# Graph layer on one core: the column lists get tiles of 128 columns of any one set of row groups, and every list product becomes 128x32

## The chip, the core and the metric

One core of a Trainium2 chip. TensorE (PE) multiplies, VectorE (DVE) adds, builds lists and normalises, ScalarE (ACT) evicts, GpSimd (POOL) issues the gathers, SyncE (SP) and ACT issue plain DMAs. The metric is the device time of one execution in microseconds (us), lower is better; a time stands for the median of several runs.

## The reference

x is 8 x 4096 x 256, adj 4096 x 4096, W 256 x 256, all f32.

```python
def reference(x, adj, W):
    HW = einsum('bnf,fo->bno', x, W)
    A_norm = relu((adj + adj.T) * 0.5)
    d = sum(A_norm, axis=1) ** -0.5                  # 0 where the sum is 0
    L_norm = eye(4096) - d[:, None] * A_norm * d[None, :]
    y = relu(einsum('nm,bmo->bno', L_norm, HW))
    return layernorm(x + y, axis=-1)
```

adj is sparse: an entry (i, j) is present with a probability that falls as (1+i)^-0.5 (1+j)^-0.5, so that low-numbered rows and columns are dense and the rest is thin. The kernel must read where the entries are; nothing of adj's pattern is known when it is built except the sizes of tables that are written into the program.

## The kernel before, in words

**Stage 1.** Blocks of 512x512 of adj are loaded (SP queue), transposed on PE (L516), added to their mirror on DVE (L520), relu'd and halved on ACT (L524), and written to a_dram (ACT queue). Sums over 32 columns (DVE L527) tell which group of 32 rows uses which column (`uses`, L528). Beside it x is transposed and multiplied by W; the rows of the result, g (8 batches x 256 = 2048 numbers, 8 KB a row), are scaled and written to g_dram. The first of 32 output blocks of 128 rows (its products are "lead" in the profile), and the lists of the first units, are also made in this stage.

**Stage 2** is the sum over neighbours. It goes through 16 units in the order `SEQ` (1 to 9, 0, 10 to 15). A unit is two output blocks of 128 rows, b = 0 and 1 (unit 15 has one), which are 8 groups of 32 rows. For each output block PE adds, in four PSUM banks (c = 0 to 3, 512 of the 2048 columns of g each), products of a tile of a (128 columns of adj x output rows) with a tile of g (those 128 rows of g). The first 256 columns of adj, the hubs, are always used whole: two hub tiles of g stay in SBUF, and a unit has 4 hub rounds (`g_hub`, `gh`), two for each block. Of the others only the columns that are used are gathered: lists of columns, cut into tiles.

In the kernel before, a list holds the columns of one of 15 fixed kinds (`KINDS`: a single group, some pairs of groups, a whole block, all eight). A list is a number of half-tiles of 64 columns (`CAPS`, `FIRST`), and a tile has two half-tiles. A round of products, which fills PE's 128 columns once for each c, is one 128x128 product, two 128x64, four 128x32, two 64x128 or up to eight 64x32 (rows of the tile x output rows). A catch-all kind takes what is left over; if it too overflows, a slower path behind the kernel runs. With these inputs that doesn't happen, in either kernel.

**The gathers.** For each tile POOL issues two indirect DMAs, `ga` from a_dram (L1032; 128 rows of 128 bytes, 512 bytes or 1 KB, depending on whether the tile serves one group, one block or both) and `g` from g_dram (L1047; up to 128 rows of 8 KB; empty places are skipped). They go into a ring of 12 tiles (`RING`). After each round the program asks for one more tile if the ring has room, for two if it has room for more than 5 (`SLACK`); these gathers wait for the round's last matmul. A ring place comes free in order only: a tile that is still in use holds all behind it. The tile order of the gathers is the order in which the rounds first use them.

**Lists.** Each unit makes steps of the lists of later units. When block 0 of a unit is finished, three of its four PSUM banks are used for counting: positions in the lists of the unit 3 and 4 ahead (L300, L301, L396, L397), and column numbers of the unit 2 ahead (`collect`, L450). DVE reads the counts (L242, L246, L247), and at the end of the unit the column numbers (`index`, L464 and L465); then the banks serve block 0 of the next unit. DVE also adds x to a finished block (L798), takes its moments (L807 to L826) and normalises it (L831); SP stores it.

The loop that orders all this, `for q, (u, step) in enumerate(steps)`, issues the products of a round, then `gather_ahead`, then list work that is due. The order on each engine is the order in which the program is written.

## Time and profile before

| what | value |
|---|---|
| runs | 1496.15, 1495.63, 1490.57 us; median 1495.63 |
| profiled execution, its own time: the span from first to last instruction (nothing lies around it that the profile shows) | 1496.2 us |
| stage 1 | 0 to 587.1 us |
| stage 2, first to last product | 587.1 to 1483.8 us |
| behind it (last block evicted, normalised, stored) | 12.4 us |
| PE / DVE / ACT / POOL busy | 1420.1 / 1025.2 / 368.7 / 745.6 us |
| bytes moved by DMA | 540.52 MB, mean 361 GB/s |

A product is two matmul instructions and two weight loads in the profile, so that a round of 128x128 is 8 matmuls. A window row gives a stretch of time, the busy time of PE, its weight loads, DVE, ACT and POOL in it with instruction counts, the granted PE clock, the mean busy share of the 16 DMA engines, and GB/s. A unit starts with the first hub product of its block 0; unit times below are from one such start to the next, in the order in which the units run:

| unit | 1 | 2 | 3 | 4 | 5 | 6 | 7 | 8 | 9 | 0 | 10 | 11 | 12 | 13 | 14 | 15 |
|---|---|---|---|---|---|---|---|---|---|---|---|---|---|---|---|---|
| us | 75.2 | 72.3 | 62.9 | 58.2 | 56.1 | 55.1 | 52.0 | 52.4 | 48.8 | 97.4 | 48.1 | 51.7 | 55.2 | 48.3 | 41.9 | 21.0 |

### The profile page before, as it was taken

To read this page: it belongs to the slowest core of one execution; us is meant where nothing else is said; L and a number is where in the kernel's file an instruction comes from. 1 tells how busy PE (TensorE), PEld (TensorE's weight loads), DVE (VectorE), ACT (ScalarE), POOL (GpSimd) and SP (SyncE) were. 2 spreads that over 40 slices of the span, in tenths; PEclk is the share of its full clock that TensorE was granted. 3 is DMA by queue.
4 is the path that set the end of the run, shared out by engine and by line. 5 is a ranking of instruction groups with operands and counts; after the bars stand their busy time and mean duration, and the time that the engine had idled before them with its cause. 6 is when DMAs were issued, how large, how long until landed. Compare 5 with 4: busy or idle time off the path is not lost.

```text
span 1496.2 us, 20479 instructions
## 1 busy us (share of the span) xinstructions
PE 1420.1 (95%) x6768; PEld 757.9 (51%) x6768; DVE 1025.2 (69%) x3010; ACT 368.7 (25%) x462; POOL 745.6 (50%) x1547
## 2 busy tenths in 40 slices
PE   7998988979999999999999999999999999998996
PEld 6777877766777764333333334333333333333342
DVE  4767558889596752356569678789898079797454
ACT  4555545434544460010100100100110011001102
POOL 2444010010322336756577677577677646666762
PEclk9999999989999999999999999999999999999998
DMA  9999999999999999979899899999999979988995
GB/s 340 360 377 381 406 346 337 393 385 338 379 356 341 371 392 373 373 270 379 332 377 379 338 402 407 366 388 403 398 382 377 387 259 341 354 316 321 402 404 220
DMA packets 215265, 540.52 MB, mean 361 GB/s; under 512 B 17751, under 2 KB 107527, under 8 KB 180839
## 3 DMA queue, kind: packets, MB, share of 16 engines
q0 software_dynamic: 53808, 281.94, 48.5%
q1 hardware_dynamic: 93200, 126.62, 24.4%
q10 hardware_dynamic: 68144, 130.58, 23.0%
q8 instruction: 56, 0.92, 0.2%
q14 instruction: 57, 0.46, 0.1%
HBM read 425.72 MB, written 136.34 MB: 376 GB/s over the span
## 4 chain that ended last, share of the span: by engine, by line
PE 62%; DMA 14%; DVE 11%; issue 7%; POOL 3%; ACT 3%; ACTq 0%; another core or an unknown queue 0%; DVEq 0%; POOLq 0%; SPq 0%
PE py L1263 45%; PE pg L627 8%; DMA a_dram<-sym 6%; DVE sym L520 4%; DMA g<-g_dram,gi 3%; PE xtr L616 3%; PE lead L585 3%; PE tr L516 3%; DMA xin<-in_x_dram 2%; POOL ga L1032 2%; ACT sym L524 1%; DVE sums L527 1%; POOL g L1047 1%; DMA g_dram<-held 1%; PE lists L450 1%
## 5 line engine op out<-in xcount | busy, mean ns | idle before, releaser
L1263 PE MATMUL py<-g,ga 128*32 128x512 f32 (+4 forms) x2880 | 644.8, 606 | 12.3 <-DMA g<-g_dram,gi 7.2
L1263 PEld LDWEIGHTS py<-g,ga 128*32 128x32 f32 (+4 forms) x2880 | 226.0, 138 | 402.0 <-issue 374.4
L1032 POOL DMA_INDIRECT ga<-a_dram,ai x256 | 277.6, 1084 | 181.3 <-issue 62.2
L1047 POOL DMA_INDIRECT g<-g_dram,gi x256 | 284.5, 1111 | 92.9 <-issue 77.6
L788 ACT ACTIVATE y<-py,minus_r 128x512 f32<-128x512 f32 x120 | 80.2, 686 | 796.3 <-PE py L1263 545.9
L627 PE MATMUL pg<-w_sb,xt 128*128 128x256 f32 x1024 | 233.4, 387 | 6.5 <-ACT xt L617 5.7
L1263 PE MATMUL py<-g_hub,gh 128*128 128x512 f32 x496 | 226.6, 601 | 0.5 <-DVE low L465 0.3
L627 PEld LDWEIGHTS pg<-w_sb,xt 128*128 128x128 f32 x1024 | 196.9, 195 | 34.5 <-ACT xt L617 6.6
L520 DVE TENSOR_TENSOR sym<-tr,adj 128x512 f32<-128x512 f32 x256 | 162.3, 684 | 59.0 <-PE tr L516 54.1
L527 DVE TENSOR_REDUCE sums<-sym 128x64 f32<-128x2048 f32 x64 | 145.7, 2282 | 69.5 <-ACT sym L524 69.5
L528 POOL TENSOR_SCALAR uses<-sums 128x64 uint8<-128x64 f32 x64 | 26.7, 417 | 271.1 <-DVE sums L527 236.9
L516 PE MATMUL tr<-ident,adj 128*128 128x128 f32 x1024 | 137.1, 281 | 20.5 <-DVE sym L520 14.3
L1263 PEld LDWEIGHTS py<-g_hub,gh 128*128 128x128 f32 x496 | 90.5, 190 | 123.6 <-issue 116.8
L524 ACT ACTIVATE sym<-sym 128x2048 f32<-128x2048 f32 x64 | 122.7, 1917 | 122.8 <-DVE sym L520 118.6
L516 PEld LDWEIGHTS tr<-ident,adj 128*128 128x128 f32 x1024 | 115.8, 143 | 50.9 <-DVE sym L520 31.1
L242 DVE TENSOR_TENSOR_SCAN incl_r<-carry,lists 128x32 f32<-128x32 bf16 x13 | 2.9, 221 | 182.0 <-PE lists L397 176.0
L429 DVE TENSOR_TENSOR hot<-iota_q,at 128x1024 bf16<-128x1024 f32 x64 | 74.5, 1220 | 34.0 <-PE lead L585 32.1
L798 DVE TENSOR_TENSOR xr<-xr,y 128x2048 f32<-128x2048 f32 x31 | 70.8, 2284 | 38.8 <-ACT y L788 32.1
L616 PE MATMUL xtr<-ident,xin 128*128 128x128 f32 x512 | 74.5, 299 | 17.9 <-DVE sym L520 9.0
L831 DVE TENSOR_SCALAR xr<-xr,mv,root 128x256 f32<-128x256 f32 x248 | 85.1, 416 | 1.1
L807 DVE BATCH_NORM_STATS2 stats<-xr 128x6 f32<-128x256 f32 x248 | 84.0, 413 | 1.1
L585 PE MATMUL lead<-gt,strip 128*128 128x512 f32 x176 | 82.4, 593 | 0.0
(164 smaller groups left out, 1040.1 us busy)
## 6 DMA issues: line engine op xcount, KB each, us to landing
adj<-in_adj_dram SPq DMA_DIRECT2D x64, 1024.0 KB
a_dram<-sym ACTq DMA_DIRECT2D x64, 1024.0 KB
out_dram<-xr SPq DMA_DIRECT2D x31, 1024.0 KB
xr<-in_x_dram ACTq DMA_DIRECT2D x28, 1024.0 KB
xin<-in_x_dram SPq DMA_DIRECT2D x44, 512.0 KB
g_dram<-gt ACTq DMA_DIRECT2D x22, 1024.0 KB
xin<-in_x_dram POOLq DMA_DIRECT2D x20, 512.0 KB
g_dram<-held ACTq DMA_DIRECT2D x10, 1024.0 KB
```

The lines of the kernel that those rows point to most:

```text
L516: ins = nc.tensor.transpose(pt[:, c * P : (c + 1) * P], tji[:, c, a * P : (a + 1) * P], ident)
L520: nc.vector.tensor_add(sym[:, a, :], pt, tij[:, a, :])
L524: nc.scalar.activation(sym, sym, AF.Relu, scale=0.5)
L527: nc.vector.tensor_reduce(sums, sym.rearrange("p a (c q) -> p a c q", q=E), AX.X, ALU.add)
L585: nc.tensor.matmul(lead[c], lhsT=strip, rhs=g[:, c * S : (c + 1) * S], start=not done, stop=len(done) == NB - 1, skip_group_check=True,)
L616: nc.tensor.transpose(pt[:, k, c, :], xin[b // H][:, b % H + k, c * P : (c + 1) * P], ident)
L627: ins = nc.tensor.matmul(pg[:, k * FO : (k + 1) * FO], lhsT=xt[:, b + k, c, :], rhs=w_sb[:, c, :], start=(c == 0), stop=(c == FC - 1),)
L807: nc.vector.bn_stats(stats[:, b, :], z[:, b, :])
L831: nc.vector.tensor_scalar(z[:, b, :], z[:, b, :], mv[:, b, 0:1], rstd[:, b : b + 1], ALU.subtract, ALU.mult,)
L1032: rows = nc.gpsimd.indirect_dma_start(out=at if both else at[:, : E if one else P], out_offset=None, in_=a_pairs if both else a_groups if ...
L1047: nc.gpsimd.indirect_dma_start(out=gt, out_offset=None, in_=g_dram, in_offset=bass.IndirectOffsetOnAxis(ap=gi[:, t : t + 1], axis=0), boun ...
L1263: return nc.tensor.matmul(py[2 * u + 1 + b][c][cols, :], lhsT=at[ps, off + cols.start : off + cols.stop], rhs=gt[ps, c * S : (c + 1) * S], ...
```

## The change

A table `UNITS` replaces `KINDS`, `CAPS`, `FIRST` and the half-tiles. For each unit it gives: how many full tiles each single group has; the other kinds, each any set of groups as a bit mask, with its number of tiles of 128 columns; the catch-all tiles; the order of the tiles (`turns`); from how many of the next tiles a round may choose (`reach`); and by how much block 1 stands back in that choice (`lag`).

```diff
-KINDS = [15, 1, 4, 2, 8, 16, 64, 32, 128, 240, 51, 204, 60, 195, 0]
-CAPS = [ ... ]
-FIRST = [ ... ]
+UNITS = [
...
+    (
+        [1, 2, 1, 1, 1, 1, 1, 1],
+        [(5, 1, 0), (64, 1, 1), (49, 1, 2), (212, 1, 3), (75, 1, 4), (186, 1, 5)],
+        1,
+        [2, 13, 11, 8, 9, 3, 14, 1, 0, 15, 4, 5, 7, 10, 12, 6],
+        7,
+        8,
+    ),
...
-    REACH = 8
-    SLACK = 5
+    SLACK = 3
-    L = 64
...
+    def match(n, u, pat, k, masks, by):
+        nc.vector.tensor_tensor(beside, pat, masks, ALU.bitwise_and)          # groups that the kind lacks
+        nc.vector.scalar_tensor_tensor(f, beside, 0.0, by, ALU.is_equal, ALU.mult)
+        nc.vector.tensor_reduce(best, f, AX.X, ALU.max)
+        nc.vector.tensor_scalar(best, best, 0.5, None, ALU.max)
+        nc.vector.tensor_tensor(kinds_in[n], f, best, ALU.is_equal)
+        nc.vector.tensor_tensor_scan(ahead_of[n], carry, kinds_in[n], 0.0, ALU.mult, ALU.add)
...
     def lists(u, room):
                 if 3 in ahead[u]:
-                    count_rest(ahead[u][3], pr[:, 0], pr[:, 1])
-                    reads.append(place_rest(ahead[u][3], pr[:, 0], pr[:, 1]))
+                    count_rest(ahead[u][3], pr)
+                    reads.append(place_rest(ahead[u][3], pr))
                 if 4 in ahead[u]:
-                    count(ahead[u][4], tot, low)
-                    reads.append(place(ahead[u][4], tot, low))
+                    count_more(ahead[u][4], q1)
+                    reads.append(place_more(ahead[u][4], q1))
+                if 5 in ahead[u]:
+                    count(ahead[u][5], q0)
+                    reads.append(place(ahead[u][5], q0))
...
     def steps_of(u):
+        out = [full(-1 - h, 0) for h in held] + ([full(-1, 1)] if two else [])
+        while any(todo.values()):
+            near = [t for t in turns if todo[t]][:reach]
+            cells = sorted((op for t in near for op in todo[t]), key=lambda op: turn[op[0]] + lag * op[1])
+            step = []
+            for j in range(QU):
+                step += [op for op in cells if op[2] == j][:1]
+            for op in step:
+                todo[op[0]].remove(op)
+            out.append(step)
+        if two:
+            out += [full(-1 - h, 1) for h in held[1:]]
...
-            for _ in range(room if behind is None else min(room, 1 + (room > SLACK))):
+            for _ in range(room if behind is None else min(room, 1 + room // SLACK)):
                 gather(asked, behind)
...
-                lhsT=at[ps, off + cols.start : off + cols.stop],
-                rhs=gt[ps, c * S : (c + 1) * S],
+                lhsT=at[:, off + cols.start : off + cols.stop],
+                rhs=gt[:, c * S : (c + 1) * S],
```

(The operands of `match` are shortened here.) A column goes to the first kind of the table that holds all its groups, in a first pass over at most 7 kinds and the single groups; what finds no place there is matched again in a second pass, and what then is left goes to the catch-all. So there are three counts for a unit's lists where there were two: 5, 4 and 3 units ahead. Constants come by one DMA from a table in the program, where 752 memsets on POOL wrote them in stage 1. The lists of the first five units are made in stage 1.

What the edit makes of each unit (columns in the lists are the same in both; MB are those columns' 8 KB rows, the `ga` rows, the hub rows, x in and the result out; "ahead" is the least number of tiles that are asked for and not yet begun behind any round of the unit, counted in the program):

| unit | columns | rounds before | after | tiles before | after | MB before | after | least ahead before | after |
|---|---|---|---|---|---|---|---|---|---|
| 1 | 2599 | 20 | 19 | 22 | 23 | 27.1 | 27.3 | 3 | 3 |
| 2 | 2325 | 17 | 17 | 20 | 20 | 24.6 | 24.8 | 6 | 4 |
| 3 | 2128 | 17 | 16 | 19 | 17 | 23.0 | 23.1 | 7 | 1 |
| 4 | 2046 | 15 | 15 | 18 | 17 | 22.2 | 22.3 | 6 | 2 |
| 5 | 1972 | 15 | 14 | 16 | 17 | 21.6 | 21.6 | 7 | 2 |
| 6 | 1855 | 15 | 14 | 15 | 16 | 20.7 | 20.5 | 7 | 4 |
| 7 | 1874 | 14 | 14 | 16 | 15 | 20.6 | 20.8 | 7 | 5 |
| 8 | 1778 | 14 | 13 | 14 | 16 | 19.9 | 19.8 | 7 | 4 |
| 9 | 1652 | 13 | 12 | 14 | 13 | 18.8 | 18.8 | 8 | 7 |
| 0 | 3000 | 27 | 23 | 26 | 24 | 30.9 | 31.1 | 7 | 4 |
| 10 | 1680 | 13 | 13 | 14 | 14 | 19.1 | 19.0 | 7 | 5 |
| 11 | 1594 | 12 | 12 | 15 | 13 | 18.1 | 18.3 | 3 | 3 |
| 12 | 1569 | 12 | 12 | 15 | 13 | 17.9 | 18.1 | 3 | 6 |
| 13 | 1537 | 12 | 12 | 13 | 13 | 17.8 | 17.7 | 6 | 5 |
| 14 | 1505 | 12 | 11 | 12 | 12 | 17.3 | 17.4 | 7 | 6 |
| 15 | 838 | 6 | 5 | 7 | 8 | 10.4 | 10.3 | - | - |
| all | 29952 | 234 | 222 | 256 | 251 | 330 | 331 | | |

In list rounds there were 1440 products, and are 2472. PE, start of unit 3 before, from the last products of its first hub round: a round of four tiles (16 products) stands between it and the second hub round, which follows 12 rows further on. (py_unit_block_c is the PSUM bank of column chunk c; g0 to g11 and ga0 to ga11 are places of the ring; g_hub0 and g_hub1 the two hub tiles.)

```order
L1263 MATMUL py_3_0_1_6884<-g_hub0_5719,gh0_0_5784 128x512
L1263 MATMUL py_3_0_2_6885<-g_hub0_5719,gh0_0_5784 128x512
L1263 MATMUL py_3_0_3_6886<-g_hub0_5719,gh0_0_5784 128x512
L1263 MATMUL py_3_0_0_6883<-g6_5751,ga6_5778 32x512
L1263 MATMUL py_3_0_0_6883<-g7_5755,ga7_5779 32x512
L1263 MATMUL py_3_0_0_6883<-g8_5759,ga8_5780 32x512
L1263 MATMUL py_3_0_0_6883<-g9_5763,ga9_5781 32x512
```

PE, start of the same unit after, from the last product of its first hub round: three hub rounds stand back to back, and then every round is of four 32-wide products.

```order
L1272 MATMUL py_3_0_3_6248<-g_hub0_4943,gh0_0_5008 128x512
L1272 MATMUL py_3_0_0_6245<-g_hub1_4947,gh1_0_5010 128x512
L1272 MATMUL py_3_0_1_6246<-g_hub1_4947,gh1_0_5010 128x512
L1272 MATMUL py_3_0_2_6247<-g_hub1_4947,gh1_0_5010 128x512
L1272 MATMUL py_3_0_3_6248<-g_hub1_4947,gh1_0_5010 128x512
L1272 MATMUL py_3_1_0_6329<-g_hub0_4943,gh0_1_5009 128x512
L1272 MATMUL py_3_1_1_6330<-g_hub0_4943,gh0_1_5009 128x512
L1272 MATMUL py_3_1_2_6331<-g_hub0_4943,gh0_1_5009 128x512
L1272 MATMUL py_3_1_3_6332<-g_hub0_4943,gh0_1_5009 128x512
L1272 MATMUL py_3_0_0_6245<-g7_4979,ga7_5003 32x512
L1272 MATMUL py_3_0_0_6245<-g8_4983,ga8_5004 32x512
L1272 MATMUL py_3_0_0_6245<-g9_4987,ga9_5005 32x512
```

What moved: the second hub round of block 0 and the first of block 1 now stand ahead of the unit's first list round, where a list round parted them; the last of block 1 stands at the unit's end. The tiles in use at one time are 3.2 on the mean over all rounds, where they were 0.9.

DVE, in unit 3, before: what stands between the counts of unit 3's banks (lists0 to lists2) and the moments of its block 0 (L798, the block numbered 7).

```order
L242 SCALAR_TENSOR_TENSOR incl_r6_7145<-carry_96,lists2_3_7140 128x32
L246 TENSOR_TENSOR pos_r6_7147<-incl_r6_7145,lists2_3_7140 128x32
L247 TENSOR_TENSOR pos_r6_7147<-pos_r6_7147,lists2_3_7140 128x32
L242 SCALAR_TENSOR_TENSOR incl_k7_7150<-carry_96,lists0_3_7138 128x448
L246 TENSOR_TENSOR pos_k7_7152<-incl_k7_7150,lists0_3_7138 128x448
L247 TENSOR_TENSOR pos_k7_7152<-pos_k7_7152,lists1_3_7139 128x448
L798 TENSOR_TENSOR xr_7_6999<-xr_7_6999,y_7_7125 128x2048
```

DVE after, the same place from its fourth row on (ahead of these stand L510 and L512, 128x32, and L480, 128x192; behind them L491, then the moments, with L493 behind their first row):

```order
L514 TENSOR_TENSOR pos1_6_6549<-lists2_3_6539,fits1_6_6547 128x32
L481 TENSOR_TENSOR wide_1_at2_7_6552<-lists1_3_6538,begin_7_6054 128x192
L482 TENSOR_TENSOR wide_0_fits2_7_6551<-wide_0_fits2_7_6551,kinds_in_1_113 128x192
L483 TENSOR_TENSOR wide_1_at2_7_6552<-wide_1_at2_7_6552,wide_0_fits2_7_6551 128x192
L485 TENSOR_REDUCE more_7_6557<-wide_1_at2_7_6552 128x32
L434 TENSOR_TENSOR wide_0_fits_8_6567<-lists0_3_6537,tables_99 128x384
L486 TENSOR_TENSOR slot_7_6199<-slot_7_6199,more_7_6557 128x32
L437 TENSOR_TENSOR wide_1_at_8_6568<-lists0_3_6537,tables_99 128x384
L488 TENSOR_SCALAR none2_7_6560<-slot_7_6199 128x32
L445 TENSOR_TENSOR begin_8_6572<-lists0_3_6537,tables_99 128x4
```

What moved: where six rows stood ahead of the moments now fourteen stand, and the column numbers (`index`, L573 and L574 now), whose bank holds up the next unit's fourth hub product, follow the moments as before.

More of the change, by code (lines that the diff above doesn't have):

```diff
@@ L204 @@
[L204 to L225 removed]
+    NT = NE + NM
@@ new lines @@
+    tiles_at = [sum(tiles[:u]) for u in range(NU)]
+    beyond = np.full((NU, NT), 1023, np.int32)
+    limits = np.zeros((NU, NT), np.float32)
+    starts = np.zeros((NU, NT), np.float32)
+    for u, (full, kinds, *_) in enumerate(UNITS):
+        at = 0
+        for g in range(NE):
+            beyond[u, g] = 1023 & ~(1 << g)
+            limits[u, g], starts[u, g] = full[g] * P, at
+            at += full[g] * P
+        for k, (mask, n, first) in enumerate(kinds):
+            beyond[u, NE + k] = 1023 & ~mask
+            limits[u, NE + k], starts[u, NE + k] = n * P, at + first * P
@@ L394, in count_rest @@
[L394 to L410 removed]
+        none = t([P, NB], "none", bufs=1)
@@ L1054, in gather @@
                 )
-            got[u, t] = (at, gt, P if both else 0, one)
+            got[u, t] = (at, gt, who)
         def gather_ahead(behind=None):
```

750 lines of the change are left out of this document (379 added, 371 removed), and 32 rows, old and new, of tables (CAPS, FIRST).

## The prediction

> **What bounds the kernel now.** I read the page first (busy shares, then the DMA tenths by slice), then windows over the two stages and over single units, then PE's groups by shape and its waits, then timelines at a few places.
>
> ```profile
> PE 1420.1 (95%) x6768; PEld 757.9 (51%) x6768; DVE 1025.2 (69%) x3010; ACT 368.7 (25%) x462; POOL 745.6 (50%) x1547
> DMA  9999999999999999979899899999999979988995
> ```
>
> PE is busy for 95% of the span, and DMA is at 90% or more in most slices. The windows say where each of them is the limit: the two stages, then units 1, 2, 7, 11 and 12, then three stretches at DMA's extremes.
>
> ```profile
> 0.00:587.10 587.10, 542.16 (x2894) 423.92 (x2895) 401.05 (x768) 280.70 (x329) 153.12 (x981) 0.97 0.99 368
> 587.10:1483.80 896.70, 877.96 (x3875) 334.00 (x3873) 618.81 (x2217) 83.03 (x125) 587.91 (x563) 0.99 0.95 361
> 587.10:662.34 75.24, 74.87 (x341) 28.18 (x340) 34.51 (x116) 4.54 (x8) 48.34 (x47) 1.00 0.84 314
> 662.34:734.68 72.34, 68.35 (x310) 25.17 (x309) 44.42 (x162) 5.25 (x9) 47.03 (x47) 1.00 0.95 358
> 966.98:1018.97 51.99, 51.62 (x248) 19.89 (x245) 44.25 (x161) 5.62 (x9) 37.90 (x35) 1.00 0.99 376
> 1265.68:1317.40 51.72, 49.85 (x249) 19.59 (x246) 40.55 (x142) 5.53 (x9) 31.33 (x30) 0.97 0.86 308
> 1317.40:1372.60 55.20, 49.48 (x244) 18.58 (x243) 42.72 (x166) 5.50 (x9) 36.38 (x35) 0.94 0.93 338
> 650.00:655.00 5.00, 4.63 (x36) 2.27 (x33) 4.52 (x7) 0.00 (x0) 0.00 (x0) 1.00 0.01 3
> 1000.00:1025.00 25.00, 24.63 (x152) 10.36 (x148) 18.36 (x83) 5.50 (x8) 18.16 (x18) 1.00 1.01 397
> 1025.00:1050.00 25.00, 25.00 (x88) 9.00 (x82) 22.95 (x66) 0.00 (x0) 16.62 (x16) 1.00 1.03 414
> ```
>
> Stage 1 runs at a DMA share of 0.99: the loads of adj set its length. Stage 2 has PE at 878 of 896.7 us and DMA at 0.95 together; neither has much to spare. DMA's full pace is the mean of the last two rows, 0.405 MB/us. Where the ring is full it stands still (share 0.01 at 650), and what it misses there can't be caught up at a pace above full.
>
> A round of products has one price, whatever its shape:
>
> ```profile
> 1018.97 3.60 PE L1263 MATMUL py<-g_hub,gh 128*128 128x512 f32 x8
> 1022.50 3.64 PE L1263 MATMUL py<-g,ga 128*32 128x512 f32 x32
> 1026.07 3.70 PE L1263 MATMUL py<-g_hub,gh 128*128 128x512 f32 x8
> 779.60 5.54 PE L1263 MATMUL py<-g,ga 64*32 64x512 f32 x32
> 784.98 0.18 PE L396 MATMUL lists<-rest,ones 128*128 128x32 bf16 x1
> ```
>
> From start to start a hub round takes 3.53 us, a round of four 128x32 3.57; I take 3.55. A 64x32 round takes 5.38 (779.60 to 784.98), 1.8 more. Unit 7 shows the rest: 51.99 - 14 rounds x 3.55 = 2.3 us for counting and collecting, which all units but the last two have.
>
> So each unit has a floor: the larger of 3.55 x rounds + 2.3 (plus 1.8 in units 1, 2, 11 and 12, for their 64x32 round with all 8 products) and its MB / 0.405. Unit 1: 20 x 3.55 + 2.3 + 1.8 = 75.1 against 27.1/0.405 = 67.0; it took 75.2. With the rounds and MB of the table the floors of before sum to 870.2. The 896.7 measured are 26.5 more, and this is not spread out: units 2, 11, 12 and 13 took 7.9, 5.0, 8.5 and 3.4 us above theirs, 24.8 together. These are the places during or behind the three units in which the least number of tiles ahead falls to 3 (units 1, 11, 12); everywhere else it is 6 or more. A dip to 3 costs 24.8/3 = 8.2 us. The reason shows at unit 12:
>
> ```profile
> 1330.86 9.86 DMA g<-g_dram,gi
> 1351.53 9.82 DMA g<-g_dram,gi
> 1347.93 9.89 PE L1263 MATMUL py<-g,ga 64*32 64x512 f32 x60 [2.80 <-DMA g<-g_dram,gi]
> PE py L1263 <- DMA g<-g_dram,gi: 7.2, 5, 2.8
> ```
>
> In the chain that ended last a gather takes 10 us from issue to landing, nearly three rounds, and then PE waits. PE's own list of waits has only 7.2 us of this; the rest is in matmuls whose modelled ends run long, and in the granted clock (0.94 in unit 12). I price it by unit times, not by waits.
>
> **The change, part by part.** *Fewer rounds.* 234 become 222, and no 64x32 is left: 12 x 3.55 + 4 x 1.8 = 50 us of PE. But in units 5, 8, 9, 11 and 14 DMA's floor now lies above PE's (unit 14: 17.4/0.405 = 43.0 against 11 x 3.55 = 39.1). The floors after sum to 827.9: a gain of 42.3, of which unit 0 alone brings 14.2 (27 to 23 rounds).
>
> *More, smaller products.* 1032 more products, 2064 more matmuls, but four to a round: by the rows above 0.04 us a round for the 128 more rounds of that shape, 5 us at most; against it 125 changes of product shape fewer, of which none shows a price. Between -5 and +5, I take 0: the 3.55 is the mean of both. The Trainium skill (TensorEngine Tiling (Array Packing), Restrictions) speaks against the change here: column tiling switches fast weight load off. By that rule the 32-wide loads would be dearer, and the sum a little above mine; the trace shows no round longer than those 0.04 us.
>
> *The ring.* This is where the gain goes. A tile now serves several rounds, each with four tiles; 3.2 are in use on the mean instead of 0.9, and a place is freed in order only. Of 12 places 7.8 are ahead instead of 8.7. Worse is the rhythm: three hub rounds back to back (10.6 us) use no tile, the ring fills to 11 or 12, POOL has nothing to ask, and DMA drains; then rounds of four new tiles come. What a full ring does is in the trace:
>
> ```profile
> 643.75 1.00 POOL L1047 DMA_INDIRECT g<-g_dram,gi  x1 [0.30 <-issue]
> 655.22 1.11 POOL L1032 DMA_INDIRECT ga<-a_dram,ai  x1 [10.46 <-PE py L1263]
> 656.63 1.00 POOL L1047 DMA_INDIRECT g<-g_dram,gi  x1 [0.30 <-issue]
> 657.93 0.95 POOL L1032 DMA_INDIRECT ga<-a_dram,ai  x1 [0.30 <-issue]
> ```
>
> POOL waits 10.46 us for a product, and then issues a tile each 2.7 us (655.22 to 657.93). A fully used tile is 1.05 MB, 2.6 us at full DMA pace, so asking faster (`SLACK` 3) gains nothing once DMA is full. Price: a dip to 3 is 8.2 us, and each tile less or more is one round, 3.55, more or less: 15.3 for 1, 11.75 for 2, 4.65 for 4, 1.1 for 5. By the table: unit 3 (1) 15.3; units 4 and 5 (2) 23.5; units 1 and 11 (3) 16.4; units 2, 6, 8, 0 (4) 18.6; units 7, 10, 13 (5) 3.3. Together 77.1, so stage 2 takes 827.9 + 77.1 = 905.0, that is +8.3. Bounds: a fixed 8.2 for each of the five dips to 3 or less (41 us, the rivals' case B), and 2.7 us for each late tile (case C). I take the graded price since its steps are those of the rounds. The Trainium skill (DMA: Bandwidth & Descriptors, Anatomy of one DMA — SWDGE (gpsimd) path) has 2.0 us + bytes / 436 GB/s for one such DMA, by which I estimate 4.4 us for a full tile. By it a tile asked two rounds ahead would be in time, the sum would be without this term; the 10 us in the chain, with several gathers sharing the engines, say otherwise.
>
> *The bank handover.* DVE stands between the counts and the next unit's hub round:
>
> ```profile
> L242 DVE TENSOR_TENSOR_SCAN incl_k<-carry,lists 128x448 f32<-128x448 bf16 x12 | 13.0, 1080 | 0.7 <-remote 0.7
> L247 DVE TENSOR_TENSOR pos_k<-pos_k,lists 128x448 f32<-128x448 f32 x12 | 7.5, 622 | 1.2
> L247 DVE TENSOR_TENSOR pos_r<-pos_r,lists 128x32 f32<-128x32 f32 x13 | 2.4, 187 | 0.4
> L370 DVE TENSOR_TENSOR more<-pos_k,upto 128x256 f32<-128x256 f32 x32 | 13.4, 420 | 0.5 <-DVE total L319 0.4
> 1074.46 1.10 PE L1263 MATMUL py<-g_hub,gh 128*128 128x512 f32 x2 [0.29 <-DVE low L465]
> ```
>
> Ahead of the moments stood 1.08 + 2 x 0.62 + 3 x 0.19 = 2.9 us. Now come two of 128x384 (0.55, between the 420 and 622 ns), five of 128x192 (0.35) and seven small ones (0.19): 4.2 us, by estimate. The column numbers thus come 1.4 us later, and PE's fourth hub product waited for them already once (0.29, unit 0). With some 0.6 us of slack elsewhere this is 0.8 in each of 14 units at the worst, 11 us; at best 0, since the hub rounds stand there anyway. I take 3. Queued behind that product are the next hub rounds, and so the gathers paced by them.
>
> *DVE and POOL otherwise.* The new match costs more in `patterns`, less in the placing; DVE had 44.25 of 51.99 us in unit 7, and unit 9 after is at 46.4: still below. Five tiles less are 5 x 2.7 us of POOL, which has 588 of 897. Both 0.
>
> *Stage 1.* 752 memsets leave POOL (153 of 587 us busy), a small table is loaded, the lists of five units are made, all beside a DMA at 0.99. 0, bounds -5 and +5 (a hundredth of the stage).
>
> Sum: -42.3 + 50.6 (77.1 - 26.5) + 3 = +11.3. The profiled execution's span is 1496.2, 0.6 above the median: 1507 us.
>
> **The rivals.**
> *A, the ring suffices.* The dips cost no more than before, 26.5: the floors' gain comes whole, 1495.6 - 42.3 = 1453. For it: PE's waits for gathers are only 7.2 us now. Against: DMA's share in stage 2 would have to be 0.95 x 896.7/854.4 = 0.997 on the mean, with pauses at full rings in each unit. Chance 0.10.
> *B, a dip has a fixed price.* Only dips to 3 or less cost, 8.2 each: 827.9 + 41 + 1.7 = 870.6, with the handover's 3 this is 1473. It ends faster, and decides where a tile two rounds late costs no more than one. DMA's share would be 0.98; unit 7 had 0.99. Chance 0.22, with 1465 to 1490.
> *C, each late tile costs.* Tiles asked four rounds or less ahead of their first use: 13 before, 37 after; four each are unit 1's first. 24.8/9 = 2.75 each, x 33 = 91 us; with the full handover of 11 stage 2 takes 930: 1529. Chance 0.20.
> *D, PE stops at each unit's start* for L574 by 3 us or more, beyond the handover's bound: 14 x 3 = 42 on top. DVE's slack in unit 7 (7.7 us) speaks against. Chance 0.03.
>
> **How the numbers follow.** 0.5% (7.5 us) is about what a measurement of this kernel tells from no change. The forecast has 0.42, with its own range 1490 to 1522: 0.10 of it within 7.5 us, 0.32 slower. A and B are faster with 0.28, 0.04 of B lies within 0.5%; 0.03 is for a gain above the floors'. C and D are slower, 0.23. Together: faster 0.31, same 0.14, slower 0.55. The range from 1460 to 1533 leaves out A and the far side of C and D, less than 0.2.
>
> **What the profile after would show.** 3.55 us from start to start in rounds of four products; unit 0 shorter by 10 us or more, as it has rounds to lose and few dips. Unit 3, 4 and 5 longer than their floors (59.1, 55.5, 53.4) by 10 us or more, with PE waiting for g behind the hub rounds, and POOL waiting for products, DMA share falling, in these. Mean share of stage 2 at 0.94 (0.95 x 896.7/908). Stage 1's end within 5 us of 587. Wrong would be a share of 0.98 and more (A or B), PE waits for g spread over all units (C), or for L574 (D).

## The result, and the profile after

The changed kernel takes 1575.26 us (median of 4 runs, 1566.32 to 1579.11) against 1495.89 us (1490.57 to 1497.34) of the kernel before on the same chip: a ratio of 1.052, interval 1.048 to 1.057. The profiled execution's span is 1577.2 us, 81.0 more than before. By stage: stage 1 ends at 596.3 for 587.1 (+9.2); stage 2, first to last product, takes 964.8 for 896.7 (+68.1); behind the last product lie 16.1 us for 12.4 (+3.7).

Windows of the kernel after, with the columns of before: the two stages, then units 1, 3, 4, 5 and 0.

```profile
0.00:596.29 596.29, 543.04 (x2904) 419.81 (x2905) 417.12 (x734) 279.18 (x329) 109.75 (x213) 0.97 0.98 361
596.29:1561.10 964.81, 872.65 (x5961) 331.28 (x5959) 581.61 (x1943) 83.33 (x126) 579.39 (x553) 0.97 0.91 339
596.29:681.41 85.12, 79.06 (x552) 34.50 (x551) 35.87 (x112) 4.36 (x8) 55.84 (x52) 1.00 0.86 319
761.34:826.84 65.50, 60.62 (x440) 20.16 (x439) 42.82 (x144) 4.02 (x7) 29.98 (x30) 0.97 0.74 273
826.84:897.44 70.60, 61.99 (x407) 23.79 (x406) 44.48 (x155) 6.98 (x11) 42.12 (x40) 0.98 0.89 328
897.44:964.39 66.95, 58.62 (x392) 19.80 (x391) 42.68 (x141) 5.50 (x9) 37.11 (x36) 0.92 0.85 313
1200.30:1293.83 93.53, 84.11 (x680) 37.41 (x679) 35.67 (x118) 4.67 (x9) 48.07 (x47) 0.95 0.84 313
```

In stage 2 PE has 873 us of work, 5 less than before, in 68 us more; DMA's share fell from 0.95 to 0.91. So neither engine is used better, and both stand idle for longer than before. Of these units, unit 3 has the lowest DMA share (0.74), unit 5 the lowest granted clock (0.92). Unit 0, with four rounds less, is 3.9 us shorter (93.5 for 97.4).

PE's longest waits, from its list of waits (microseconds in total, times, longest):

```profile
PE py L1272 <- DMA g<-g_dram,gi: 48.4, 24, 4.0
PE py L1272 <- issue: 12.2, 23, 2.3
PE q L409 <- DVE ahead_of L362: 12.1, 1, 12.1
PE lists L559 <- DVE fits L512: 11.8, 3, 9.4
PE lists L559 <- DVE pos L514: 8.0, 5, 5.7
PE py L1272 <- DVE low L574: 0.6, 1, 0.6
```

The wait for gathers went from 7.2 us in 5 places to 48.4 in 24. The 12.1 us are one wait in stage 1, for DVE's new scan. The wait for L574 at a unit's start came once. The counts (L559) wait for L512 and L514.

The chain that ended last has a round of four products in 3.57 us, as before, and a gather of 10.5 us (start, length):

```profile
1074.26 3.57 PE py L1272 x32
1164.60 10.51 DMA g<-g_dram,gi
```

From POOL's timeline, in unit 1, and then from PE's, in units 1 and 5 (start, length, what ran, the idle time before it and its releaser):

```profile
633.04 0.95 POOL L1041 DMA_INDIRECT ga<-a_dram,ai  x1 [6.93 <-PE py L1272]
```

```profile
614.87 1.02 PE L1272 MATMUL py<-g,ga 128*32 128x512 f32 x2 [0.80 <-issue]
616.31 1.02 PE L1272 MATMUL py<-g,ga 128*32 128x512 f32 x2 [0.42 <-issue]
617.76 1.04 PE L1272 MATMUL py<-g,ga 128*32 128x512 f32 x2 [0.43 <-issue]
621.32 32.27 PE L1272 MATMUL py<-g,ga 128*32 128x512 f32 x284 [0.82 <-issue]
954.08 6.59 PE L1272 MATMUL py<-g,ga 128*32 128x512 f32 x26 [4.03 <-DMA g<-g_dram,gi]
```

POOL's row is the full ring: it has nothing to ask for 6.9 us. PE's first three are something else: one product each 1.45 us (614.87, 616.31, 617.76), where four should run together in 0.9, and PE waits for nothing that the profile shows. The row at 621.32 has the proper pace: 284 matmuls are 35 and a half times 8, 32.3 us. The last row is unit 5: 4 us for a tile that was asked too late. The window that begins with it shows what follows, PE at half its clock (0.50) for 3.4 us:

```profile
954.08:957.49 3.41, 3.41 (x16) 0.79 (x20) 1.63 (x6) 0.00 (x0) 0.25 (x1) 0.50 0.89 303
```

### The profile page after: what moved, and what is told of

Same layout as the page of the kernel before. It is cut to its first block, busy times and chain, and to the rows that moved or that the text cites. A ratio compares the mean times of both kernels' runs of the same rounds, so it can differ in the third digit from the quotient of the medians.

```text
span 1577.2 us, 23550 instructions
## 1 busy us (share of the span) xinstructions
PE 1415.7 (90%) x8864; PEld 751.1 (48%) x8864; DVE 1004.1 (64%) x2702; ACT 367.5 (23%) x462; POOL 694.9 (44%) x771
## 4 chain that ended last, share of the span: by engine, by line
PE 34%; issue 10%; POOL 8%; DMA 7%; another core or an unknown queue 6%; DVE 6%; ACT 1%; POOLq 0%; ACTq 0%; DVEq 0%
PE py L1272 27%; DMA g<-g_dram,gi 5%; POOL ga L1041 4%; POOL g L1056 3%; PE lead L692 3%; PE pg L734 2%; DVE stats L916 1%; DMA a_dram<-sym 1%; DVE xr L907 1%; DMA ga<-a_dram,ai 1%; PE lists L559 1%; DVE hot L534 1%; PE tr L623 0%; DVE xr L940 0%
## 5 line engine op out<-in xcount | busy, mean ns | idle before, releaser
L1272 PE MATMUL py<-g,ga 128*32 128x512 f32 x4944 | 633.4, 610 | 62.8 <-DMA g<-g_dram,gi 48.4
L1272 PEld LDWEIGHTS py<-g,ga 128*32 128x32 f32 x4944 | 219.9, 112 | 446.9 <-issue 408.6
L1041 POOL DMA_INDIRECT ga<-a_dram,ai x251 | 263.6, 1050 | 275.1 <-PE py L1272 160.0
L1056 POOL DMA_INDIRECT g<-g_dram,gi x251 | 289.8, 1155 | 94.8 <-issue 75.8
L734 PE MATMUL pg<-w_sb,xt 128*128 128x256 f32 x1024 | 229.3, 382 | 3.5 <-ACT xt L724 3.5
L1272 PE MATMUL py<-g_hub,gh 128*128 128x512 f32 x496 | 220.0, 600 | 3.1 <-ACT y L897 2.6
L510 DVE TENSOR_SCALAR over<-lists 128x1 f32<-128x1 f32 x13 | 2.1, 159 | 279.4 <-remote 88.0
L623 PE MATMUL tr<-ident,adj 128*128 128x128 f32 x1024 | 140.5, 283 | 21.9 <-DVE sym L627 19.3
L1272 PEld LDWEIGHTS py<-g_hub,gh 128*128 128x128 f32 x496 | 93.5, 192 | 118.8 <-issue 107.3
L692 PE MATMUL lead<-gt,strip 128*128 128x512 f32 x176 | 86.7, 614 | 0.0
L724 ACT COPY xt<-xtr 128x512 f32<-128x512 f32 x128 | 67.7, 593 | 75.7 <-PE xtr L723 74.9
```

Source lines behind the costliest of these rows:

```text
L623: ins = nc.tensor.transpose(pt[:, c * P : (c + 1) * P], tji[:, c, a * P : (a + 1) * P], ident)
L692: nc.tensor.matmul(lead[c], lhsT=strip, rhs=g[:, c * S : (c + 1) * S], start=not done, stop=len(done) == NB - 1, skip_group_check=True,)
L734: ins = nc.tensor.matmul(pg[:, k * FO : (k + 1) * FO], lhsT=xt[:, b + k, c, :], rhs=w_sb[:, c, :], start=(c == 0), stop=(c == FC - 1),)
L1041: rows = nc.gpsimd.indirect_dma_start(out=at[:, :width], out_offset=None, in_={2: a_pairs, ALONE: a_groups}.get(who, a_rows), in_offset=ba ...
L1056: nc.gpsimd.indirect_dma_start(out=gt, out_offset=None, in_=g_dram, in_offset=bass.IndirectOffsetOnAxis(ap=gi[:, t : t + 1], axis=0), boun ...
L1272: return nc.tensor.matmul(py[2 * u + 1 + b][c][cols, :], lhsT=at[:, off + cols.start : off + cols.stop], rhs=gt[:, c * S : (c + 1) * S], s ...
```

## The experiments

The runs were made in several sets, each on one chip and beside the kernel before. In two of the sets that kernel takes 1471 us, in the others, and in the first comparison above, 1495 to 1500; ratios are therefore compared within a set, or between sets of one kind. In the sets of 1471, PE's list of waits has no wait for nothing visible ("issue") in front of a product of stage 2, and steps like that of 614.87 are hardly there; the others have both, in both kernels. "Short" and "long" sets below are these two. Tiles asked late, that is four rounds or less ahead of their first use, are counted in the program.

### Set 1 (short, before 1471.95): is it the products, the ring, or the bytes?

b_split: the kernel before, with each list product of 128 rows split into products of 32 columns (2776 list products for 1440).

```diff
-                    cols = slice(op[3] * E, (op[3] + op[4]) * E)
-                    ins = product(u, op, c, rows, cols, first, op in last)
+                    width = op[4] if op[0] < 0 or op[1] is not None else 1
+                    for e in range(op[3], op[3] + op[4], width):
+                        cols = slice(e * E, (e + width) * E)
+                        ins = product(u, op, c, rows, cols, first, op in last)
```

> The kernel before, with each list product of 128 rows that is 64 or 128 wide issued as two or four products of 32 columns in the same round (2776 list products instead of 1440; the changed kernel has 2472). Rounds, tiles, ring and lists stay. Theory I (PE is short of instructions when a round is 64 of them: rounds that wait for nothing visible run long): it loses what the changed kernel loses there, 50 us or more, 1540 to 1580. Theory R (the ring: held tiles, freed in order, let DMA run dry and PE wait for g): nothing of the ring changes, 1496 within 8.

b_ring10: the kernel before with `RING = 10` for 12, so that 61 tiles are late where 13 were.

> The kernel before with a ring of 10 tiles instead of 12: 6.8 tiles ahead on the mean (8.7 before, 7.8 after the change), 61 tiles asked four rounds or less ahead of their first use (13 before, 37 after). Theory R: it is worse off than the changed kernel in both counts and loses at least what that loses to the ring, 1540 to 1580. Theory I: the ring has little to do with it, under 1515.

a_half and b_half: the two kernels with gathers of 4 KB a row for 8; of each row of g only the first half is fetched, and the products use it twice, so the second half of g's columns is left out.

```diff
-                    out=gt,
+                    out=gt[:, : G // 2],
...
-                    in_=g_dram,
+                    in_=g_dram.rearrange("j (h q) -> (j h) q", h=2),
...
-                    rhs=gt[:, c * S : (c + 1) * S],
+                    rhs=gt[:, c % 2 * S : (c % 2 + 1) * S],
...
```

> The changed kernel with gathers of 4 KB rows instead of 8 KB (the second half of g's columns is left out; products of the first half stand in for it), everything else as it was. The bytes that the gathers move are halved, the instructions are the same. Theory R: waits for g go (48 us) and with them the lowered clock, 1500 or less. Theory I with a supply that is slow by itself: rounds that wait for nothing visible stay long, some 55 us, so 1490 to 1510 and 0.7 us steps between single products in the timeline. Theory I with a supply that is slow since it shares the DMA engines with the gathers: these go too, 1440 to 1465.

> The kernel before with the same halved gathers: what PE and the lists alone allow there. By the floors stage 2 takes 234 x 3.55 + 14 x 2.3 + 7 = 870 us instead of 896.7: 1470 by all theories; the difference to the changed kernel with halved gathers is then the change without DMA: 50 us less for the change if only rounds count, and more than before if list steps or instructions hold PE up.

Measured: b_split 1473.44, ratio 1.001 (0.999 to 1.003); b_ring10 1543.48, 1.049 (1.045 to 1.053); a_half 1472.49, 1.000 (0.997 to 1.003); b_half 1459.35, 0.992 (0.988 to 0.995). The windows of stage 2 in b_split, then in b_ring10, and the latter's wait for gathers:

```profile
579.42:1453.28 873.86, 859.94 (x6547) 286.69 (x6545) 618.05 (x2217) 85.32 (x125) 590.65 (x562) 1.00 0.97 371
```

```profile
581.01:1529.38 948.37, 897.90 (x3875) 337.51 (x3873) 611.73 (x2210) 85.29 (x125) 578.49 (x564) 0.97 0.92 342
```

```profile
PE py L1263 <- DMA g<-g_dram,gi: 45.1, 23, 4.3
```

In a short set the smaller products cost 1.5 us, within what can be told from no change. Two ring places less do to the kernel before much what the change does in a short set (a_again, below): 1.049 for 1.043, waits for gathers of 45.1 us in 23 places for 63.7 in 36, DMA's share 0.92 for 0.94, the clock 0.97 in both. 48 more late tiles cost 74.5 us of stage 2 against b_split, 1.6 each. With half the bytes to fetch, the change still costs 13 us (1472.49 - 1459.35), and that is in stage 1 (its end at 597.5 for 581.1), where the halved gathers have no part. Stage 2 is then 4 us shorter with the change (860.0 for 864.1), not the 43 of twelve rounds at 3.55 us: PE still waits 30.6 us for gathers in 22 places. The halved rows take 57 us from the changed kernel's stage 2 (917.3 in a_again), so bytes and late asking work together.

### Set 2 (short, before 1470.85): which part of the ring?

a_again is the changed kernel unaltered. a_free gives a ring place back as soon as its tile has no more products, in any order:

```diff
+        places, place_of = list(range(RING)), {}
...
-            at, gt = ring_rows[n % RING], ring[n % RING]
+            place_of[n] = places.pop(0)
+            at, gt = ring_rows[place_of[n]], ring[place_of[n]]
...
-            while eaten < asked and not uses_left[order[eaten]]:
-                eaten += 1
-            room = min(len(order), eaten + RING) - asked
+            for k in sorted(place_of):
+                if not uses_left[order[k]]:
+                    places.append(place_of.pop(k))
+            room = min(len(order) - asked, len(places))
...
```

> The changed kernel as it is, beside the others of this set. Ratio to before 1.04 to 1.055: by theory R all of it comes from the ring and the waits that follow (clock, lists), plus about 10 us in stage 1. If steps of 0.7 us between single products, which the first pair of profiles has and the last four have not, are a part of the loss (theory I), the ratio is 1.03 to 1.04 where they are missing.

> The changed kernel with ring places freed in any order: a tile that is still in use holds its own place only. 9.4 tiles ahead on the mean instead of 7.8, 4 tiles asked four rounds or less ahead instead of 37; rounds, products and tile order stay. Theory R (freeing in order is what starves it): 55 to 85 us less than the changed kernel, at most 1.00 of before. If the burst after three hub rounds without new tiles is the cause, and not the places: less than 25 us less.

a_spread sets the hub rounds of a unit apart (before the first list round, behind it, and so on) instead of three in a row.

> The changed kernel with its hub rounds put apart as before: a list round behind the first hub round, block 1's first hub round only ahead of its first list round. Freed in order: 7.2 tiles ahead, 47 asked four rounds or less ahead (37 in the changed kernel). By the counts of theory R it is no better than the changed kernel, or up to 15 us worse. If three hub rounds back to back, with a full ring and idle DMA, are the cause, 25 to 50 us better.

a_stage1 moves the first count of each of stage 1's lists one block on, so that PE does not stand before L409.

```diff
-                    due += [[at + k, fn, (u,)] for k, fn in enumerate(whole[:upto])]
+                    due += [[at + k + (k > 0), fn, (u,)] for k, fn in enumerate(whole[:upto])]
```

> The changed kernel with each unit's first count in stage 1 issued one block later than its match, so that PE needn't wait for DVE's scan (12 us at 312 us of the profile). If that wait is what makes stage 1 longer: 8 to 12 us less than the changed kernel. If DVE's load of five matches beside the sums is what makes it longer: no change, within 4.

Measured: a_again 1532.75, 1.043 (1.040 to 1.046); a_free 1461.57, 0.993 (0.991 to 0.995); a_spread 1543.58, 1.050 (1.047 to 1.053); a_stage1 1535.10, 1.043 (1.040 to 1.045). Stage 2 and the wait for gathers, a_again first, then a_free:

```profile
597.42:1514.72 917.30, 850.31 (x5961) 295.60 (x5959) 581.02 (x1943) 85.27 (x125) 582.83 (x552) 0.97 0.94 356
```

```profile
PE py L1272 <- DMA g<-g_dram,gi: 63.7, 36, 3.5
```

```profile
597.02:1447.58 850.56, 821.85 (x5961) 286.49 (x5959) 579.68 (x1943) 85.28 (x125) 590.04 (x553) 0.99 1.00 384
```

```profile
PE py L1276 <- DMA g<-g_dram,gi: 25.6, 20, 3.1
```

This is the main cause of what the change loses in a short set. With the order of release alone altered, late tiles fall from 37 to 4, stage 2 from 917.3 to 850.6 and the whole to 0.7% below the kernel before. Of the 66.7 us, 38.1 are waits for g (63.7 less 25.6), and 28.5 lie in PE's busy time for the same products (850.3 less 821.9), with the clock at 0.97 for 0.99. 66.7 us for 33 late tiles are 2.0 each on the mean, but half of it lies in units 3, 4 and 5, which have eleven of the late tiles: together 202.0 us in a_again, 168.3 in a_free.

```profile
750.27:952.23 201.96, 179.08 (x1235) 61.70 (x1234) 132.08 (x445) 16.49 (x25) 111.39 (x106) 0.96 0.84 313
```

```profile
743.12:911.46 168.34, 165.53 (x1236) 57.26 (x1235) 128.92 (x427) 16.51 (x25) 112.28 (x109) 0.99 0.99 375
```

DMA is at 1.00 for all 850 us of a_free's stage 2, and its pace, held so long, is 384 GB/s.

a_spread is slower still: the hub rounds in a row are not what hurts. The program has 47 late tiles with them apart, since a round without a new tile then comes where the ring has room; stage 2 took 928.1, 11 more. a_stage1 took its wait away (12.1 to 0.4 us) and the end of stage 1 came 3.6 us sooner, but the total did not move: in the profiled execution stage 2 took 6.6 us longer (923.9 for 917.3), for a cause that no run shows.

### Set 3 (long, before 1496.53): stage 1's lists, and bytes and ring together

a_free_late is a_free with the lists of the third, fourth and fifth unit made later in stage 1 (blocks 20, 26, 31 for 15, 22, 28). a_free_half is a_free with 4 KB gathers, as in a_half, the second half of g's columns again left out. b_ring11 is the kernel before with `RING = 11` (29 late tiles).

> The changed kernel with places freed in any order (as in a_free), and in stage 1 the lists of the third, fourth and fifth unit begun 5, 4 and 3 blocks later, so that the third unit's steps no longer meet the column lists (hot, L534) of the first on DVE between 300 and 360 us, where DVE is busy for 59.4 of 60 us. If that burst is what makes stage 1 16 us longer than before: 6 to 15 us less than a_free, ratio to before 0.982 to 0.989. If something else in stage 1 does: within 4 us of a_free, ratio 0.993.

> a_free with gathers of 4 KB rows (the second half of g's columns is left out, as in the other halved kernels). In a_free DMA's share is 1.00 over all of stage 2 (850.6 us at 384 GB/s). If DMA's bytes are what is left there: stage 2 falls to PE's floor, 222 x 3.55 + 14 x 2.3 = 820, up to 830, so 1430 to 1442 in all. If POOL's pace, PE's instructions or the lists hold it: 1450 or more.

> The kernel before with a ring of 11: 7.8 tiles ahead on the mean, as in the changed kernel, but 29 asked four rounds or less ahead of their first use (37 in the changed kernel, 13 before, 61 with a ring of 10). With a ring of 10 each late tile more cost 1.55 us (74 us for 48). If late tiles count: 25 us more than before, ratio 1.017. If the mean number ahead counts: as much as the changed kernel loses in stage 2, 43 us, ratio 1.03. If neither: within 0.5%.

Measured: a_free_late 1521.35, 1.020 (1.014 to 1.026); a_free_half 1510.51, 1.010 (1.006 to 1.015); b_ring11 1507.49, 1.008 (1.005 to 1.011). Stage 2 of a_free_half, and PE's waits for nothing visible in it:

```profile
595.66:1491.68 896.02, 851.09 (x5961) 304.85 (x5959) 581.22 (x1943) 80.45 (x125) 562.02 (x554) 0.99 0.75 229
```

```profile
PE py L1276 <- issue: 18.1, 37, 0.8
```

A kernel with a free ring, a DMA that is busy for three quarters and no wait for g at all takes 896 us in a long set. Its 222 rounds would be 788 at 3.55 us, 820 with 2.3 us for counting and collecting in each of 14 units. So something other than the ring and the bytes holds it. What the short sets do not have are the "issue" rows and some waits of the counts for DVE (5.6 us for L512, 4.8 for L480 in this run). The later lists brought nothing: stage 1 ends at 594.7, in a_free2 and a_free3 below at 595.9 and 594.4. b_ring11 cost 11.0 us for 16 more late tiles, 0.7 each, where 25 us were expected from the step to ten places in the short set: a price per late tile is not a constant.

### Set 4 (long, before 1500.17): the number of instructions

b_split2 and a_free2 are b_split and a_free again, in this kind of set. a_free_pair is a_free with neighbouring columns of a round given to the same tile where it is near, and joined to one 128x64 (or 128x128) product: 1876 list products for 2472.

```diff
...
+            for j in (0, 2):
+                if j in by and j + 1 in by and by[j][:2] == by[j + 1][:2]:
+                    out.append((*by[j][:3], 2))
+                else:
+                    out += [by[k] for k in (j, j + 1) if k in by]
...
```

> The kernel before with its 1440 list products cut into 2776 of 32 columns, as in b_split, here to be read by whether the profiles of this set show steps of 0.7 us. If they do, and the number of instructions makes them (theory I): 40 to 80 us more than before, ratio 1.03 to 1.055. If they do and the number has nothing to do with them: within 0.5% of before. If they don't: 1.000 as in the set before.

> a_free again. Where the steps show: like a_free_late in the set before, ratio 1.015 to 1.025 by theory I (27 less than the changed kernel's 1.052: the ring's share). Where they don't: 0.993.

> a_free, with two neighbouring columns of a round given to the same tile and block where the tile has both and the cell is near its turn, and such products joined to one of 64 columns: 1876 list products instead of 2472 (before 1440), the same 160 list rounds, 4 tiles asked four rounds or less ahead. Where the steps show, theory I: a third to a half of what b_split loses to them comes back against a_free, 20 to 35 us, ratio to before 0.995 to 1.01. Where they don't: as a_free, 0.99 to 0.995.

Measured: b_split2 1529.11, 1.021 (1.015 to 1.028); a_free2 1515.35, 1.013 (1.006 to 1.020); a_free_pair 1704.05, 1.137 (1.130 to 1.145). Stage 2 of b_split2, a row of its PE timeline in unit 1, and its waits for nothing visible; then stage 2 and these waits of a_free2:

```profile
585.66:1515.01 929.35, 901.14 (x6547) 317.06 (x6545) 619.29 (x2217) 82.21 (x125) 586.37 (x562) 1.00 0.92 348
```

```profile
605.67 3.54 PE L1263 MATMUL py<-g,ga 128*32 128x512 f32 x7 [0.80 <-issue]
```

```profile
PE py L1263 <- issue: 12.0, 24, 0.8
```

```profile
595.95:1496.88 900.93, 851.69 (x5961) 304.58 (x5959) 581.63 (x1943) 80.97 (x125) 567.50 (x553) 0.99 0.97 363
```

```profile
PE py L1276 <- issue: 17.9, 37, 1.9
```

The split that cost 1.5 us in a short set costs 29 here, at a granted clock of 1.00 and with DMA at 0.92, that is, with neither of them at its limit. In the row at 605.67, seven matmuls take 3.5 us, the time of a whole round of 32. The same kernel with a free ring needs 50 us more in stage 2 than in the short set (900.9 against 850.6). What a long set lacks is products in time, and a kernel that has more of them loses more: in stage 2 a long set takes 55.5 us more of b_split (2776 list products), 50.3 of a_free (2472), and some 23 of the kernel before (1440; 896.7 for the 873.9 of b_split, since no profile of it was taken in a short set). The DMA queue that the profile names "instruction" shows no difference between the kinds: 73 packets, 1.20 MB, 0.3% of the DMA engines' time in a_free and in a_free2.

a_free_pair tells something else. Its product groups by shape:

```profile
L1302 PE MATMUL py<-g,ga 128*32 128x512 f32 x2896 | 486.5, 599 | 0.0
L1302 PE MATMUL py<-g,ga 128*64 128x512 f32 x688 | 301.3, 614 | 0.0
```

344 products of 64 columns take 301 us of PE, 0.88 each, where two of them should run side by side, 0.45 each. 62 of its rounds mix a 64-wide product with 32-wide ones. In these the widths run one after the other. Half of such a round, two of the four banks (4 matmuls of 64 columns, 8 of 32), is this row:

```profile
601.39 4.04 PE L1302 MATMUL py<-g,ga 128*64 128x512 f32 x12
```

That is 4 us where a whole round takes 3.6. At 3.55 us more each, 62 such rounds are 220 us by estimate; 197 more than a_free2 were measured (1097.5 - 900.9), and it had fewer of the slow steps to lose. So the gain that was expected of fewer products could not show here.

### Set 5 (long, before 1494.89): the ring taken out of both, and even rounds

b_free is the kernel before with a_free's release in any order, a_free3 the same kernel as a_free. a_free_even joins products only where a whole round becomes one 128x128, two 128x64, or one 128x64 alone; 1952 list products, no mixed round, 6 late tiles.

> The kernel before, with ring places freed in any order, as a_free has them. Theory (the ring freed in order cost the change some 67 us, because its tiles serve several rounds; before, a tile serves about one round, and only 13 are asked late): little to win, 13 late tiles x 0.7 to 2 us, so 9 to 25 us at the very most, ratio 0.985 to 1.00. Rival (any-order places help every kernel alike, so that the change with a free ring gains nothing beside it): 40 us or more, ratio below 0.975.

> The changed kernel with the ring free, a third time, beside b_free on the same chip. Where the kernel before takes about 1471: 0.993 of it. Where it takes about 1496 to 1500 and products run in steps of 0.7 us that wait for nothing: 1.01 to 1.02. What the change is worth with the ring taken out of both kernels is this ratio over that of b_free.

> a_free with products joined only where the whole round becomes one 128x128 or two 128x64 (or one 128x64 alone), so that no round mixes widths; 160 list rounds as before, 1952 list products for 2472; 6 late tiles for 4. Theory (rounds that mix widths cost 3.55 us more each, and small products cost where their supply is late): no jump as in a_free_pair (1.137). On a chip with the 0.7 us steps the fifth of products that goes takes back a fifth to a half of the 50 us: ratio 0.99 to 1.005. On a chip without them the same as a_free, 0.993. Rival (every change of product width inside stage 2 costs): slower than a_free by 20 us or more on either chip.

Measured: b_free 1481.86, 0.992 (0.989 to 0.995); a_free3 1515.06, 1.015 (1.012 to 1.018); a_free_even 1504.20, 1.006 (1.004 to 1.009). PE's waits for nothing visible in a_free3 and in a_free_even, and the latter's list products by shape:

```profile
PE py L1276 <- issue: 13.5, 27, 0.9
```

```profile
PE py L1305 <- issue: 8.7, 15, 1.8
```

```profile
L1305 PE MATMUL py<-g,ga 128*32 128x512 f32 x3408 | 432.0, 604 | 9.7 <-issue 5.3 <-DMA g<-g_dram,gi 2.7
L1305 PE MATMUL py<-g,ga 128*64 128x512 f32 x224 | 54.7, 615 | 1.6 <-issue 1.6
```

The kernel before gains 13 us from the free ring, where the changed one gained 71 in a short set (a_free against a_again): most of what a_free takes back is the change's own loss, not all. Stage 2 of a_free3, then of b_free:

```profile
594.38:1495.23 900.85, 851.97 (x5961) 310.89 (x5959) 582.03 (x1943) 81.25 (x125) 566.05 (x554) 0.98 0.97 363
```

```profile
581.54:1471.29 889.75, 875.79 (x3875) 334.95 (x3873) 617.31 (x2217) 82.44 (x125) 587.81 (x563) 0.99 0.96 363
```

With both rings free, in one long set, the change still makes stage 2 11.1 us longer.

520 products fewer take 10.9 us off a_free3, and the waits fall from 13.5 to 8.7. Changes of width between rounds show no cost; a 64-wide product now takes 0.49 us (54.7/112), side by side, against 0.88 in a_free_pair: mixing widths inside a round was what cost.

The best version of all depends on the set: in a short one a_free (0.993), in a long one b_free (0.992), each less than 1% below the kernel before. b_free was not run in a short set.

## Why the prediction was right and wrong

The prediction forecast 1507 us, slower by 11, from a gain in rounds that the ring gives back. The direction came true, and the ring cost about what it said; the time, 1575, lies 42 us above its range. The step that failed is the gain from fewer rounds, -42.3 with nothing put down for smaller products. With the ring taken out of both kernels (a_free3 and b_free), the change makes stage 2 11 us longer, where the terms other than the ring (-42.3, 0 and +3) make it 39 shorter. These 50 us are most of the 57 by which stage 2 was missed (68.1 for 11.3). By its own steps:

**Fewer rounds, -42.3: mis-sized.** The rounds' price held (3.57 us in the chain of after, 284 matmuls in 32.3 us). Two figures beside it did not. The first is the 1.8 us more for a round of 64x32 products, which is a row misread. The row of 779.60 begins inside such a round, at the edge of the window that was asked for, and runs on into the round behind it; what PE does from 780 to 784.9 is

```profile
L1263 PE MATMUL py<-g,ga 128*128 128x512 f32 x8 | 3.7, 605 | 0.0
L1263 PE MATMUL py<-g,ga 64*32 64x512 f32 x24 | 1.9, 589 | 0.0
```

half a round of 64x32 products and a whole one of 128x128. Without the 1.8 the gain would have been 35.

The second is DMA's floor: "full pace 0.405 MB/us" was the mean of two windows of 25 us at their best. Held for 850 us at a share of 1.00 the pace is 0.384. With that, DMA's floor lies above PE's in 15 units of 16 after the change, and the gain is 23. (The prediction's sums leave unit 15 at PE's price, though its DMA floor, 25.7 us, is above PE's 21.3. By the rule as stated its gain was 39.1, and with both corrections it is 20.) On the chip a_free's stage 2 is 23.3 below b_split's in a short set (850.6 and 873.9); of this some 7 may be the ring of before (b_free).

Unit 0, whose PE floor lies above DMA's at either pace, shows that the rounds themselves paid: 82.3 us in a_again, the changed kernel unaltered, for 98.3 in b_split, both in short sets.

```profile
1173.27:1255.52 82.25, 82.05 (x679) 28.98 (x678) 40.61 (x140) 5.49 (x9) 50.45 (x50) 1.00 0.95 367
```

```profile
1097.69:1195.98 98.29, 97.20 (x792) 31.05 (x788) 44.18 (x161) 5.50 (x8) 58.95 (x58) 1.00 0.91 338
```

That is the 14.2 of the forecast and more. In the first comparison, of the long kind, only 3.9 of it are left.

**The ring, +50.6: the mechanism right, the size near, in part by luck.** Of the 77.1 us put down for dips, 66.7 are shown (a_again less a_free) in a short set and 63.9 in the long kind (964.8 of after less 900.9 of a_free2, in different sets). Units 3, 4 and 5, the deepest dips, lost 33.6 us where the table gave them 38.8. But 26.5 was subtracted for dips of before; its ring is worth 7 to 13 us by b_free (896.7 to 889.8 in stage 2, 1494.9 to 1481.9 in all). So the term was 50 to 60, and the remainder of stage 2 in the long kind (68.1 - 11.1) is 57.

The luck is in the price of a dip. It was taken from 24.8 us that units 2, 11, 12 and 13 took above their floors before the change, and unit 2's 7.9 of these were hardly a dip. One of its rounds, of eight small products for each bank (64 matmuls), took 11.4 us (707.11 to 718.54), and 3.6 in b_half, in a short set. The round in the kernel before, then in b_half:

```profile
L1263 PE MATMUL py<-g,ga 64*32 64x512 f32 x64 | 8.8, 597 | 2.6 <-issue 2.4
```

```profile
L1263 PE MATMUL py<-g,ga 64*32 64x512 f32 x64 | 3.7, 592 | 0.0
```

That three hub rounds in a row make the dips worse was not borne out (a_spread). Rival C, one price for each late tile, is right that each costs: 2.0 us on the mean in a_free against a_again, below its 2.75. But it was 0.7 in b_ring11 (in a long set, where other waits may cover some of it), and in the short set some 3 in units 3 to 5, so the price is not fixed. Behind the waits the granted clock falls (0.50 behind the wait of 4.03 us, 0.92 in all of unit 5), which no term had.

**More, smaller products, 0 between -5 and +5: wrong in long sets.** The bound was taken from rounds that ran well (3.57 against 3.53 us). Its experiment, b_split, gave 1.5 us where before takes 1471, as told, and 29 where it takes 1500. For the change itself some 27 us of stage 2 come from this: a_free takes 50.3 more in a long set than in a short one, the kernel before 23. The sign of it stood in the profile of before and was not read: the round of 11.4 us above, with "issue" as the end of its waits. In b_half the same round takes 3.6 us, so it is no property of the shape. By the rule on fast weight load that the prediction cites from the Trainium skill (TensorEngine Tiling (Array Packing), Restrictions) the 32-wide loads would cost in every set; b_split's 1.5 us in the short set speaks against this as the cause.

**Stage 1, 0 between -5 and +5: wrong.** It ended 9.2 us later in the first comparison, 13 later in set 5 (594.4 and 581.5), and 18 later in short sets (597.0 and 579.4). A window of a_free at 340 us, then at 360, and the same two of b_split:

```profile
340.00:360.00 20.00, 20.00 (x111) 15.49 (x110) 19.94 (x26) 10.34 (x14) 2.49 (x3) 1.00 0.88 323
360.00:380.00 20.00, 15.16 (x65) 10.96 (x64) 12.15 (x25) 4.44 (x5) 1.07 (x2) 0.83 0.72 275
```

```profile
340.00:360.00 20.00, 16.41 (x83) 11.46 (x82) 18.88 (x42) 7.93 (x10) 2.52 (x4) 1.00 0.94 350
360.00:380.00 20.00, 19.97 (x141) 15.77 (x140) 17.00 (x59) 8.97 (x11) 6.49 (x11) 1.00 0.92 337
```

DVE has no idle time (19.94 of 20) while it makes the new lists, nor has PE, and DMA's share falls to 0.72 behind it. "Beside a DMA at 0.99" was the cover that the term named; DVE adds each block to its mirror, and where it is late the blocks' writes are. That the list work is the cause is argued from these rows, not shown: moving the count (a_stage1) brought 3.6 us of stage 1 back, later lists (a_free_late) nothing, and neither made the whole shorter.

**The bank handover, +3, and DVE and POOL, 0: right or near.** L574 was waited for once, 0.6 us; rival D did not come. But in long sets the counts wait for L512 and L514 (11.8 and 8.0 us), work of DVE that was put at 0 as long as its busy share stayed below PE's.

**The sum as measured**, for the first pair, each part from the sets named above: +9 for stage 1; in stage 2 +57 for the ring (of the change, less that of before) and +11 for the rest, in which a gain of some 16 from fewer rounds (the 23.3 less 7) stands against some 27 that only long sets have; +4 behind the last product, not followed up. Together 81.

**What the profile after was to show:** rounds of 3.55 us and units 3, 4 and 5 longer than their floors (by 6.4, 15.1 and 13.6 us; for unit 3 less than told) came; unit 0's ten came in the short set alone, stage 1's end within 5 us did not; the DMA share of stage 2 is 0.91 for 0.94. Waits for g in units beyond those three were named as the sign of C, and they were there too.

## What to carry to other kernels

When a tile begins to serve several rounds, look at how its buffer comes free before counting rounds: a ring that frees in order lost 67 us here, and ten lines that free in any order took it back. Take an engine's full pace from the longest stretch in which it never waited, not from its best 25 us. Before a row of a merged timeline becomes a price, ask for the matmuls in it by shape: a row can begin in the middle of a round. And a round's price measured where all goes well is no bound for rounds with two or four times the instructions: read the waits for nothing visible ("issue") in the profile of before, shape by shape.

## What the runs showed of the hardware that was not expected

- The same program has two speeds in its many-product rounds, by set: single products 0.7 or 1.4 us apart for stretches of some microseconds, with the operands there and the clock at 1.00. b_split costs 0.1% in one kind of set and 2.1% in the other. Fewer products help (a_free_even, 10.9 us). A late supply of PE with instructions is the likely name for it, since more is lost where there are more of them; no run shows that by itself, and what makes a set short or long stays open. The record has chip 7 for set 1, a short one, and for set 5, a long one, so if the number means the same chip both times, the chip alone does not decide it.
- Products of different width in one round of the same PE columns do not run side by side: 128x64 beside 128x32 took two rounds' time (62 such rounds, 197 us). Two of 128x64, or four of 128x32, do (0.49 us a 64-wide product in a_free_even, 0.88 in a_free_pair).
- PE's granted clock falls behind waits of a few microseconds: 0.50 for 3.4 us behind the wait of 4.03 us in unit 5, 0.92 over that unit, against 1.00 in unit 1. A wait for a tile thus costs more than its own length.
- A late gather costs on the mean between 0.7 us (b_ring11) and 2.0 us (a_free against a_again), far less than the 10 us that it takes to land.
